# L1's context keys made before L0's expert tiles, and fewer buffers in L1's self-attention

## The chip, the cores and the metric
The kernel runs on one core of a Trainium2 chip. Its metric is device time in microseconds of one execution. Five engines work side by side: PE multiplies matrices into PSUM (its weight loads are shown as PEld), DVE and ACT work on vectors and empty PSUM, POOL does vector work and issues indirect (gathering and scattering) DMAs, and SP issues the plain DMAs. Each engine takes its instructions strictly in the order of its own queue, and waits for the others by semaphores.

## The reference
A decoder of four layers, L0 to L3, is applied to x (8 sequences of 256 tokens, width 256, f32) with a context of 8 x 77 tokens of width 256. Each layer is self-attention, cross-attention and a feed-forward part, each added to x and followed by a layer norm:

```
x = _layernorm(x + _L0_xattn_ref(x, ctx_1024, ...), axis=-1)   # 16 heads of 64
x = _layernorm(x + _L0_ffn_ref(x, ...), axis=-1)               # 8 experts, top 2
x = _layernorm(x + _L1_attn_ref(x, ...), axis=-1)              # 16 heads of 16, causal
x = _layernorm(x + _L1_xattn_ref(x, ctx_1024, ctx_1024, mask_BxSxS2_bk1, ...), axis=-1)  # 16 heads of 64
```

What matters here: the keys of L1's cross-attention are `ctx @ Wk + bk`, 1024 features for 616 context tokens. They depend on inputs alone and not on x, so they can be made at any time. The other stages (L1_ffn, L2, L3) are not touched.

## The kernel before, in words
All activations stay in on-chip memory: x as 16 tiles of 128 tokens (`X`), its transpose as 4 blocks of 512 tokens (`XT`), the transposed context as `cT` (128 x 2 x 616). The stages run one after the other in program order, each opening its own memory pools and closing them at its end, so a later stage's tiles lie on memory of an earlier one. A framework tracks the tiles, adds the semaphore waits, and settles the order of instructions within each engine's queue; a planned program has one fixed order per engine. Results of a batch that need not be finished at once are put on a list (`later`) and advanced by `tick` while the next batch is worked on; `settle` finishes them.

Weights go through one ring of five buffers (`load_w`, tag "w", L172): a load waits until the buffer five loads earlier is no longer read. The plain loads are issued on SP's queue. PSUM is a ring of eight banks (`ps`).

The stages around the change are these.

*L0's cross-attention* (`cross64`, L827) loads Wk, Wq, Wv and Wo, makes the keys `kT` (L839 to L850: sixteen groups of two products `ps<-cT,w` 128x308, each emptied by DVE or ACT in turn), then takes the eight batches: queries (8 groups of 128x256), scores (L894), softmax, weighing, output product, layer norm, and for each batch the routing to experts.

*L0's expert stage* (`l0_ffn`, L1133) settles the last batch's routing, then `route.tables` (L2577) counts tokens per expert with a product on PE (`rbefore,onesb`) and works the tables out on DVE. With these POOL fetches, by indirect DMA, each tile's weights (`W1`, `W2`, in the ring of five) and its 256 token rows (`gx`); PE transposes the rows (L1073), DVE copies them to `gT`, and PE does the two expert products, with the gelu on ACT between them (L1115, after a table load).

*L1's self-attention* (`l1_attn`, L1210) first clears padded tiles by POOL (L1225 to L1228): four `mxp` tiles (two per parity of the batch) and two `vp` tiles. Meanwhile expert results are gathered (`gy`, L1055), added to x (L2680) and normalised (L182 and L183 on POOL, L255 on DVE). For each batch it makes queries, keys and values, the maxima by query (L1285, into `mxp`), transposes them (L1292) and adds them to the queries (`q2`, L1294), makes the scores by key (L1304, L1307), the exponentials `e` (L1312), and weighs the values with them (L1326) into `oT`, which is emptied by L141 or L143 and taken on by `heads_out` (L1354 onwards). The maxima of the next batch are made before the weighing of this one.

*L1's cross-attention* is `cross64` again, with a bias and a mask: Wk, Wq, Wv and Wo are loaded, the keys are made with their bias (L848: `copy_bias`, DVE L148 and ACT L150 in turn), then the batches follow, with the mask (`mk`, loaded by SP, L887) applied to the scores by L908.

Of the kernel before, what the change touches and what calls it, by code (L numbers as in the profile page):

```python
# [14 lines left out]
AF = mybir.ActivationFunctionType  # L15
# [5 lines left out]
P = 128  # L21
NB = 8
S = 256
# [5 lines left out]
NC = NB * SC  # L29
# [32 lines left out]
class Build:  # L62
    def __init__(self, tc, a, ctx):
        self.tc, self.nc, self.a = tc, tc.nc, a
        self.n = 0
        self.flip = 0
        pool = lambda name, bufs=1, **kw: ctx.enter_context(tc.tile_pool(name=name, bufs=bufs, **kw))
        self.const = pool("const")
        self.xp = pool("xp", 2)
        self.wp = pool("wp", 5)  # L70
        self.sm = pool("sm", 4)
        self.tmp = pool("tmp", 3)
        self.psp = pool("ps", 8, space=PSUM)
        self.dr = pool("dr", 1, space=DRAM)
        self.open_keep = lambda: pool("keep")
        self.keep = None
        self.X = [None] * NT
        self.XT = [None] * NBLK
        self.late = lambda: pool("late")
        self.l3w = None  # L80
        self.n_slot_sets = 0
        self.todo = []
        self.results = None
        self.routed = None
        self.slots = {}
        self.ms = {}
# [737 lines left out]
            self.settle()  # L824


    def cross64(self, pre, bias, mask, row, route):  # L827
        nc, a = self.nc, self.a
        with ExitStack() as ctx:
            w1 = ctx.enter_context(self.tc.tile_pool(name=pre + "1", bufs=1))  # L830
            w2 = ctx.enter_context(self.tc.tile_pool(name=pre + "2", bufs=2))
            w3 = ctx.enter_context(self.tc.tile_pool(name=pre + "3", bufs=3))
            Wk = self.load_w(a[pre + "_Wk"], 2, 1024)
            Wq = self.load_w(a[pre + "_Wq"], 2, 1024)
            Wv = self.load_w(a[pre + "_Wv"], 2, 1024)
            Wo = self.load_w(a[pre + "_Wo"], 8, 256)
            kT = self.t(w1, [P, 8, NC], "kT")
            hc = NC // 2
            for n in range(8):  # L839
                for hf in range(2):  # L840
                    ps = self.ps()
                    self.mm(
                        ps[:, :hc],
                        [(Wk[:, k, n * P : (n + 1) * P], self.cT[:, k, hf * hc : (hf + 1) * hc]) for k in range(2)],
                    )
                    o = kT[:, n, hf * hc : (hf + 1) * hc]
                    if bias:
                        self.copy_bias(o, ps[:, :hc], self.fm("l1x_bk")[:, n : n + 1])  # L848
                    else:
                        self.copy(o, ps[:, :hc])  # L850
            if mask is not None:
                big = self.t(w1, [P, 1], "big")
                nc.vector.memset(big, -8.0e9)
# [279 lines left out]
    def l0_ffn(self, route):  # L1133
        nc, a = self.nc, self.a
        with ExitStack() as ctx:
            w1 = ctx.enter_context(self.tc.tile_pool(name="l0f1", bufs=1))
            w2 = ctx.enter_context(self.tc.tile_pool(name="l0f2", bufs=2))
            b2 = self.t(w1, [8, D], "b2")
            nc.sync.dma_start(b2, a["L0_ffn_b2"])
            self.settle()  # L1140
            route.tables(N0)

            cT = self.t(w1, [8, NT, P], "combT")

            def biased(i):
                po = self.ps()
                for k in range(2):
                    nc.tensor.matmul(po[:, k * D : (k + 1) * D], cT[:, i + k, :], b2, start=True, stop=True)
                for k in range(2):
                    nc.vector.tensor_tensor(self.X[i + k], po[:, k * D : (k + 1) * D], self.X[i + k], ALU.add)  # L1150

            def each(j):
                if j == 1:
                    route.places()
                if j == 3:
                    comb = route.combined(w1)
                    for i in range(0, NT, 4):
                        ps = self.ps()
                        for k in range(4):
                            nc.tensor.transpose(ps[:8, k * P : (k + 1) * P], comb[:, i + k, :], self.ident)  # L1160
                        nc.vector.tensor_copy(cT[:, i : i + 4, :], ps[:8].rearrange("p (k n) -> p k n", k=4))
                if j in (4, 5):
                    biased(2 * (j - 4))

            self.routed_tiles(w2, lambda: w2, U0, N0, route, "L0_ffn", 8, 8, AF.Gelu_apprx_tanh, False, True, each)
            self.collect(route)
            for i in range(4, NT, 2):
                biased(i)
# [41 lines left out]
    def l1_attn(self):  # L1210
        nc, a = self.nc, self.a
        with ExitStack() as ctx:
# [5 lines left out]
            self.slot_rows(2)  # L1218
            bk, bq = self.fm("l1_bk"), self.fm("l1_bq")

            mxps, vps = [], []
            for n in range(2):
                mxps.append([self.t(w1, [P, 4, 4, 32], f"mxp{n}{t}") for t in range(2)])
                for m in mxps[n]:
                    nc.gpsimd.memset(m, 0.0)  # L1225
                v = self.t(w1, [P, 2, H, 32], f"vp{n}")
                nc.gpsimd.memset(v, 0.0)
                nc.gpsimd.memset(v[:, :, :, 16:17], 1.0)  # L1228
                vps.append(v)
# [38 lines left out]

            def shift(b, q, k):

                q2 = self.t(w2, [P, 4, S], "q2")
                for t in range(2):
                    n = P * (t + 1)
                    mxp = mxps[b % 2][t]
                    for gs in ((0, 1, 2, 3),) if t == 0 else ((0, 1), (2, 3)):
                        ps = mats(gs, n)
                        for j in range(4):
                            nc.tensor.matmul(ps[j], self.identb, many(later[:, 2 * P - n :], len(gs)), start=True, stop=False)
                        for i, g in enumerate(gs):
                            for j, r in enumerate(rows):  # L1280
                                nc.tensor.matmul(
                                    ps[j][:, i, :], q[r, g, t * P : (t + 1) * P], k[r, g, :n], start=False, stop=(g == gs[-1])
                                )
                        for j in range(4):
                            self.mark = nc.vector.tensor_reduce(  # L1285
                                mxp[:, gs[0] : gs[-1] + 1, j, 16], ps[j], AX.X, ALU.max, negate=True
                            )
                        self.tick()
                for t in range(2):
                    pt = self.ps().rearrange("p (g s) -> p g s", g=4)  # L1290
                    for g in range(4):
                        nc.tensor.transpose(pt[:, g, :], mxps[b % 2][t][:, g].rearrange("p j d -> p (j d)"), self.ident)  # L1292
                    c = slice(t * P, (t + 1) * P)
                    nc.vector.tensor_tensor(q2[:, :, c], pt, q[:, :, c], ALU.add)  # L1294
                return q2

            def weights(q2, k):

                e = {}
                for c, gs in ((0, (0, 1)), (0, (2, 3)), (1, (0, 1, 2, 3))):  # L1300
                    n = S - c * P
                    ps = mats(gs, n)
                    for j in range(4):
                        nc.tensor.matmul(ps[j], self.causb, many(unit[:, :n], len(gs)), start=True, stop=False)  # L1304
                    for i, g in enumerate(gs):
                        for j, r in enumerate(rows):
                            nc.tensor.matmul(  # L1307
                                ps[j][:, i, :], k[r, g, c * P : (c + 1) * P], q2[r, g, c * P :], start=False, stop=(g == gs[-1])
                            )
                    o = self.t(w2, [P, 4, len(gs), n], "e", bufs=4)  # L1310
                    for j in range(4):
                        nc.scalar.activation(o[:, j], ps[j], AF.Exp, scale=0.25)  # L1312
                    for i, g in enumerate(gs):
                        e[c, g] = o[:, :, i, :]
                    self.tick()
                return e

            def weigh(b, e, v):
                o = self.t(w2, [P, 4, S], "oT")
                for gp in range(2):  # L1320
                    ps = self.ps().rearrange("p (g s) -> p g s", g=2)
                    for i in range(2):
# [1379 lines left out]
def build(tc, a, out, layers=LAYERS):  # L2702
    with ExitStack() as ctx:
# [4 lines left out]
        for l in layers:  # L2708
            if l in ("l0_xattn", "l1_xattn", "l2_xattn"):
                route = Routing(g, int(l[1]))  # L2710
            if l == "l1_ffn":
                l2k = ctx.enter_context(ExitStack())
                g.l2k_pool = l2k.enter_context(tc.tile_pool(name="l2k", bufs=1))
# [8 lines left out]
            elif l in ("l2_xattn", "l0_ffn", "l1_ffn", "l2_ffn"):  # L2722
                getattr(g, l)(route)
            else:
                getattr(g, l)()
            if l == "l2_xattn":
                l2k.close()
            if l == "l3_attn":
# [162 lines left out]
```

## Time and profile before
| | us |
|---|---|
| median of 3 runs | 3623.32 (3618.66 to 3629.59) |
| the profiled execution's own time | 3594.94 |
| its span, first to last instruction | 3593.2 |
| PE busy | 3102.3 (86%) |
| DVE busy | 1834.9 (51%) |
| ACT busy | 1043.6 (29%) |
| POOL busy | 928.1 (26%) |

The mean granted clock of PE over the span is 0.896. In the profile a group or instruction has its engine, its source line, the tiles it writes and reads (`out<-in`), partitions by elements, and the idle time before it with what ended that wait. An f32 product shows as several instructions. In the span, L0's cross-attention begins at 456 us, L0's expert tiles at 786, L1's self-attention at 1087 and L1's cross-attention at 1361. The granted clock (PEclk) is the share of full speed that PE was given in a stretch.

### The profile page before, as it was taken

To read this page: it belongs to the slowest core of one execution; us is meant where nothing else is said; L and a number is where in the kernel's file an instruction comes from. 1 tells how busy PE (TensorE), PEld (TensorE's weight loads), DVE (VectorE), ACT (ScalarE), POOL (GpSimd) and SP (SyncE) were. 2 spreads that over 40 slices of the span, in tenths; PEclk is the share of its full clock that TensorE was granted. 3 is DMA by queue.
4 is the path that set the end of the run, shared out by engine and by line. 5 is a ranking of instruction groups with operands and counts; after the bars stand their busy time and mean duration, and the time that the engine had idled before them with its cause. 6 is when DMAs were issued, how large, how long until landed. Compare 5 with 4: busy or idle time off the path is not lost. (4 is left out here: it accounts for less than half of the span.)

```text
span 3593.2 us, 49384 instructions
## 1 busy us (share of the span) xinstructions
PE 3102.3 (86%) x19146; PEld 2184.7 (61%) x19146; DVE 1834.9 (51%) x4823; ACT 1043.6 (29%) x2343; POOL 928.1 (26%) x1398
## 2 busy tenths in 40 slices
PE   4777589979997998998999999898787997778789
PEld 3444257658875665666555777565555785566556
DVE  7888546631116555776211221566675344677652
ACT  4666322212222332332111111344222111343311
POOL 2222513243314101222000000411343444312351
PEclk6777689979998999988999999999777998888889
DMA  9900100035541000001010333200002552000000
GB/s 338 305 2 1 48 7 19 19 108 181 179 144 47 1 25 25 13 14 60 15 36 0 119 124 119 62 1 8 7 19 83 198 196 77 22 1 7 12 5 19
DMA packets 132127, 239.47 MB, mean 67 GB/s; under 512 B 14568, under 2 KB 103920, under 8 KB 124208
## 3 DMA queue, kind: packets, MB, share of 16 engines
q1 hardware_dynamic: 107632, 136.25, 11.3%
q0 software_dynamic: 23104, 98.95, 7.9%
q8 instruction: 154, 2.52, 0.3%
q10 hardware_dynamic: 1152, 1.05, 0.1%
q14 instruction: 85, 0.70, 0.1%
HBM read 156.52 MB, written 79.69 MB: 66 GB/s over the span
## 5 line engine op out<-in xcount | busy, mean ns | idle before, releaser
L155 PE MATMUL ps<-xt,w 128*128 128x256 f32 (+1 forms) x1408 | 452.9, 472 | 3.3 <-issue 2.9
L155 PE MATMUL ps<-w,hT 128*128 128x256 f32 (+1 forms) x1792 | 397.4, 379 | 0.0
L155 PEld LDWEIGHTS ps<-w,hT 128*128 128x128 f32 (+1 forms) x1792 | 329.9, 186 | 56.5 <-issue 6.0
L155 PE MATMUL ps<-gT,w 128*128 128x256 f32 (+1 forms) x1472 | 357.4, 401 | 5.7 <-ACT gT L143 3.0
L155 PEld LDWEIGHTS ps<-xt,w 128*128 128x128 f32 x1408 | 268.7, 198 | 149.4 <-issue 125.0
L155 PEld LDWEIGHTS ps<-gT,w 128*128 128x128 f32 x1472 | 276.5, 191 | 76.8 <-ACT gT L143 3.9
L155 PE MATMUL ps<-w,oT 128*128 128x256 f32 x768 | 181.9, 390 | 3.3 <-DVE mv L251 1.8
L267 POOL TENSOR_TENSOR xb<-x,rows 128x256 f32<-128x256 f32 x96 | 71.6, 752 | 401.7 <-DVE res L272 393.7
L155 PEld LDWEIGHTS ps<-w,oT 128*128 128x128 f32 x768 | 146.4, 194 | 38.5 <-issue 14.1
L235 PE MATMUL ps<-ident,x 128*128 128x128 f32 x320 | 62.0, 307 | 79.5 <-DVE x L255 59.4
L1115 ACT ACTIVATE hT<-ps,more 128x256 f32<-128x256 f32 x152 | 71.9, 474 | 196.1 <-PE ps L155 196.1
L255 DVE TENSOR_SCALAR x<-res,mv,rs 128x256 f32<-128x256 f32 x128 | 57.4, 449 | 126.9 <-POOL rs L183 126.9
L1126 DVE COPY y<-ps 128x512 f32<-128x512 f32 x41 | 28.3, 690 | 174.7 <-PE ps L155 174.7
L1184 DVE TENSOR_TENSOR hT<-hT,ps 128x512 f32<-128x512 f32 x56 | 38.5, 688 | 154.2 <-PE ps L155 152.7
L677 ACT ACTIVATE e<-ps,nm 128x128 bf16<-128x128 f32 (+1 forms) x256 | 103.9, 458 | 40.1 <-DVE nm L672 24.1
L932 PE MATMUL ps<-ident,P 128*77 128x128 f32 x512 | 90.0, 303 | 25.5 <-POOL P L923 15.7
L1666 POOL TENSOR_TENSOR kpad<-kpad,rows 128x256 f32<-128x256 f32 (+1 forms) x10 | 7.3, 729 | 404.2 <-DVE hu L1615 316.9
L923 POOL TENSOR_TENSOR P<-P,z 128x1232 f32<-128x1232 f32 x24 | 54.1, 2252 | 219.6 <-DVE z L921 214.3
L183 POOL TENSOR_TENSOR rs<-rs,mhalf 128x1 f32<-128x1 f32 x192 | 106.1, 554 | 14.2
L932 PEld LDWEIGHTS ps<-ident,P 128*77 128x77 f32 x512 | 60.7, 157 | 73.4 <-issue 25.5
L947 PE MATMUL ps<-PT,V 77*64 77x256 f32 x512 | 98.5, 446 | 7.5 <-DVE PT L141 4.9
L1180 ACT ACTIVATE hT<-ps 128x512 f32<-128x512 f32 x56 | 33.4, 597 | 237.5 <-PE ps L155 237.5
(655 smaller groups left out, 6319.2 us busy)
## 6 DMA issues: line engine op xcount, KB each, us to landing
l2x<-zero SPq DMA_DIRECT2D x28, 1024.0 KB, 11.3
l0x<-zero SPq DMA_DIRECT2D x16, 1024.0 KB, 11.3
w<-in_L_ffn_rg SPq DMA_DIRECT2D x8, 1024.0 KB, 7.0
w<-in_L_ffn_ru SPq DMA_DIRECT2D x8, 1024.0 KB, 5.0
w<-in_L_ffn_rd SPq DMA_DIRECT2D x8, 1024.0 KB, 5.7
l2e<-y SPq DMA_DIRECT2D x22, 256.0 KB, 2.3
rows<-in_rows SPq DMA_DIRECT2D x9, 544.0 KB, 3.7
l0e<-y SPq DMA_DIRECT2D x19, 256.0 KB, 2.9
```

The lines of the kernel that those rows point to most:

```text
L155: self.nc.tensor.matmul(out, lhsT, rhs, start=(i == 0), stop=(i == last))
L183: self.nc.gpsimd.tensor_tensor(out, out, self.mhalf[: in_.shape[0], :w], ALU.pow)
L235: self.nc.tensor.transpose(ps[:, k * P : (k + 1) * P], x[:, k * P : (k + 1) * P], self.ident)
L255: nc.vector.tensor_scalar(t, r, mv[:, 0:1], rs, ALU.subtract, ALU.mult)
L267: self.nc.gpsimd.tensor_tensor(t, self.X[i], row, ALU.add)
L677: nc.scalar.activation(e[:, : (t + 1) * P], ps[j][:, i, :], AF.Exp, bias=nm[:, t, h : h + 1], accum_out=z[:, t, h : h + 1],)
L923: eng.tensor_tensor(pr, pr, z.unsqueeze(2).to_broadcast([P, H, SC]), ALU.mult)
L932: nc.tensor.transpose(psv[:, m, t * P : (t + 1) * P], Pt[t][:, 2 * n + m, :], self.ident)
L947: nc.tensor.matmul(po[64 * m : 64 * m + 64, :S], V[:, h * 64 : (h + 1) * 64], ahead[n % 2][:, m, :], start=True, stop=True,)
L1115: nc.scalar.activation(hT[:, f + m, :], ps[:, m * 256 : (m + 1) * 256], func, bias=more[:, f + m : f + m + 1])
L1180: nc.scalar.activation(hT[:, f, :], ps, func, **({"bias": bias(f)} if bias else {}))
L1184: nc.vector.tensor_tensor(hT[:, f, :], hT[:, f, :], ps, ALU.mult)
```

## The change
The keys of L1's cross-attention are made at the start of L0's expert stage, after the routing tables' instructions in program order, into a tile `l1kT` (128 x 8 x 616 f32, 19.7 KB a partition). It has a pool of its own, open from before L0's expert stage until the end of L1's cross-attention. All sixteen groups are emptied by ACT, with the bias; DVE takes no part. L1's Wk is loaded right after L0's four cross-attention weights, as a fifth load in the ring. L1's cross-attention neither loads Wk nor makes keys.

To make room, L1's self-attention has fewer buffers: one pair of `mxp` tiles instead of two pairs, one `q2` instead of two, three `e` instead of four, one `oT` instead of two.

```diff
+    def context_keys(self, kT, Wk, copy):
+        hc = NC // 2
+        for n in range(8):
+            for hf in range(2):
+                c = slice(hf * hc, (hf + 1) * hc)
+                ps = self.ps()
+                self.mm(ps[:, :hc], [(Wk[:, k, n * P : (n + 1) * P], self.cT[:, k, c]) for k in range(2)])
+                copy(kT[:, n, c], ps[:, :hc], *([self.fm("l1x_bk")[:, n : n + 1]] if kT is self.l1kT else []))
...
     def cross64(self, pre, bias, mask, row, route):
-            Wk = self.load_w(a[pre + "_Wk"], 2, 1024)
+            Wk = self.load_w(a[pre + "_Wk"], 2, 1024) if not bias else None
...
+            if bias:
+                kT = self.l1kT
+            else:
+                kT = self.t(w1, [P, 8, NC], "kT")
+                self.context_keys(kT, Wk, self.copy)
+                self.l1wk = self.load_w(a["L1_xattn_Wk"], 2, 1024)
...
     def l0_ffn(self, route):
             route.tables(N0)
+            self.l1kT = self.t(self.l1k_pool, [P, 8, NC], "l1kT")
+            self.context_keys(
+                self.l1kT, self.l1wk, lambda o, ps, bias: nc.scalar.activation(o, ps, AF.Identity, bias=bias)
+            )
...
     def l1_attn(self):
-            mxps, vps = [], []
+            mxps, vps = [self.t(w1, [P, 4, 4, 32], f"mxp{t}") for t in range(2)], []
+            for m in mxps:
+                nc.gpsimd.memset(m, 0.0)
             for n in range(2):
-                mxps.append([self.t(w1, [P, 4, 4, 32], f"mxp{n}{t}") for t in range(2)])
-                for m in mxps[n]:
-                    nc.gpsimd.memset(m, 0.0)
...
-                q2 = self.t(w2, [P, 4, S], "q2")
+                q2 = self.t(w2, [P, 4, S], "q2", bufs=1)
-                    mxp = mxps[b % 2][t]
+                    mxp = mxps[t]
...
-                    o = self.t(w2, [P, 4, len(gs), n], "e", bufs=4)
+                    o = self.t(w2, [P, 4, len(gs), n], "e", bufs=3)
...
-                o = self.t(w2, [P, 4, S], "oT")
+                o = self.t(w2, [P, 4, S], "oT", bufs=1)
...
     def build(tc, a, out, layers=LAYERS):
+            if l == "l0_ffn":
+                l1k = ctx.enter_context(ExitStack())
+                g.l1k_pool = l1k.enter_context(tc.tile_pool(name="l1k", bufs=1))
...
+            if l == "l1_xattn":
+                l1k.close()
```

In the planned order of the changed kernel the 32 key products stand on PE behind the count product of the tables and ahead of the first expert tile's transposes; on ACT the 16 evictions stand behind the last routing exponential and ahead of the table load for gelu. On SP, L1's Wk follows L0's Wo, and in L1's cross-attention the first load of L1_ffn (sg) moves ahead of the first two masks. On POOL, tile 2's second weight fetch moves behind tile 4's row gathers, and at the start of L1's self-attention the order of memsets, powers (L183) and gathers is a little different. Apart from these, and from the places of a few small DVE instructions, each engine's order is the same.

More of the change, by code (lines that the diff above doesn't have):

```diff
@@ L82, in __init__ @@
         self.todo = []
+        self.l1kT = None
         self.results = None
@@ L836, in cross64 @@
             Wo = self.load_w(a[pre + "_Wo"], 8, 256)
[L837 to L850, printed above, removed]
+            if bias:
[4 more added lines that the diff above has]
+                self.l1wk = self.load_w(a["L1_xattn_Wk"], 2, 1024)
             if mask is not None:
@@ L1291, in shift @@
                     for g in range(4):
-                        nc.tensor.transpose(pt[:, g, :], mxps[b % 2][t][:, g].rearrange("p j d -> p (j d)"), self.ident)
+                        nc.tensor.transpose(pt[:, g, :], mxps[t][:, g].rearrange("p j d -> p (j d)"), self.ident)
                     c = slice(t * P, (t + 1) * P)
```

## The prediction
> **What bounds the kernel now.** I read the page's head first (span 3593.2 us, PE busy 86%). The chain that ended last gives PE only 8% and does not reach back to the stages changed here, so I went by stretches: the timeline around the start of L1's cross-attention, where the keys are made now, then around the start of L0's expert tiles, where they go, then L1's self-attention between them.
>
> Timeline, start of L1's cross-attention (start, duration, engine, line, operation, idle before it):
> ```profile
> 1361.05 0.20 PEld L235 LDWEIGHTS ps<-ident,x 128*128 128x128 f32 x2 [1.25 <-PE ps L235]
> 1361.33 18.44 PE L155 MATMUL ps<-cT,w 128*128 128x308 f32 x64
> ...
> 1376.70 0.54 DVE L148 TENSOR_SCALAR kT<-ps,fmt 128x308 f32<-128x308 f32 x1 [1.54 <-PE ps L155]
> 1377.74 0.52 ACT L150 ACTIVATE kT<-ps,fmt 128x308 f32<-128x308 f32 x1 [1.55 <-PE ps L155]
> ...
> 1379.61 7.07 PE L155 MATMUL ps<-xt,w 128*128 128x256 f32 x32
> ...
> 1386.61 3.65 PEld L894 LDWEIGHTS ps<-kT,qT 64*128 64x128 f32 x64 [0.33 <-DVE qT L148]
> ```
> PE works through the keys without a break; DVE and ACT wait for it. The queries of batch 0 (x32) follow at once and the scores behind them: here PE alone sets the time.
>
> Timeline, start of L0's expert tiles:
> ```profile
> 767.28 0.19 PE L155 MATMUL ps<-rbefore,onesb 128*128 128x8 bf16 x1 [0.16 <-DVE rbefore L2538]
> ...
> 783.48 0.45 PE L1073 MATMUL ps<-ident,gx 128*128 128x128 f32 x1 [16.01 <-DMA gx<-l0x,trows]
> ...
> 785.34 0.69 DVE L1080 COPY gT<-ps 128x512 f32<-128x512 f32 x1 [11.35 <-PE ps L1073]
> ...
> 786.09 9.06 PE L155 MATMUL ps<-gT,w 128*128 128x256 f32 x28 [0.79 <-DVE gT L1080]
> ...
> 788.32 1.28 ACT L1115 ACT_TABLE_LOAD   x1 [23.59 <-PE ps L155]
> ```
> PE stands still for 16.0 us between the counts of the routing tables and the first gathered rows; ACT has nothing for 23.6 us.
>
> Busy time by stretch, the key block of L0's cross-attention (459-463) and that of L1's (1362-1368) among them (PE, PEld, DVE, ACT, POOL, then PEclk, DMA share, GB/s):
> ```profile
> 459.00:461.00 2.00, 2.00 (x6) 1.37 (x5) 0.48 (x1) 0.03 (x1) 0.00 (x0) 0.60 0.00 0
> 461.00:463.00 2.00, 2.00 (x9) 1.48 (x8) 0.48 (x1) 0.39 (x1) 0.00 (x0) 1.00 0.00 0
> ...
> 735.00:740.00 5.00, 5.00 (x24) 3.89 (x24) 1.54 (x3) 0.74 (x2) 0.00 (x0) 0.50 0.00 0
> ...
> 1362.00:1365.00 3.00, 3.00 (x7) 1.98 (x6) 0.54 (x1) 0.00 (x0) 0.00 (x0) 0.50 0.15 60
> 1365.00:1368.00 3.00, 3.00 (x13) 2.17 (x12) 0.54 (x1) 1.03 (x2) 0.00 (x0) 0.98 0.00 0
> ...
> 786.10:803.20 17.10, 17.10 (x69) 14.57 (x70) 0.69 (x1) 4.92 (x9) 10.37 (x11) 0.84 0.78 282
> 803.20:817.40 14.20, 14.20 (x69) 12.32 (x68) 1.38 (x2) 3.80 (x8) 6.80 (x8) 1.00 0.60 205
> ```
> After a pause the granted clock is 0.50 and comes back to 1.00 after about 4 us of dense work; expert tile 0 takes 17.1 us, tile 1 14.2 us.
>
> Timeline, start of L1's self-attention:
> ```profile
> 1080.94 0.51 POOL L1225 MEMSET mxp<- 128x512 f32 x1
> 1081.01 1.95 DVE L255 TENSOR_SCALAR x<-x,mv,rs 128x256 f32<-128x256 f32 x1 [1.53 <-POOL rs L183]
> 1081.40 0.94 POOL L1227 MEMSET vp<- 128x1024 f32 x1
> 1082.30 0.51 POOL L1225 MEMSET mxp<- 128x512 f32 x1
> ```
> The normalisation that PE waits for takes 1.95 us here instead of 0.41, until POOL's memsets pause.
>
> **Part 1, the keys leave L1's cross-attention.** Sixteen groups of two f32 products (x64 with their passes) go. At full clock a group takes 1.036 us (evictions at 1376.70 and 1377.74), 16 x 1.036 = 16.6; the block takes 18.3 because it began at clock 0.50 (18.3 - 16.6 = 1.7 lost, the price of 3.4 us at half clock). That slow start is inherited by the queries, so I take **-16.6**. Ends: -18.3 if the queries start at full clock; -15.5 if they stay slow for 5.6 us, as expert tile 0 did (786.1 to 791.7), losing 2.8 instead of 1.7. What could be late next: Wq landed long before (issued 1068.71); the mask is issued at 1356.93 and lands in 1.7 us, and its reader moves from 1388.2 to about 1371.6. In SP's queue L1_ffn's first load (sg) now goes ahead of the masks, but it waits for the self-attention's Wv buffer, free at 1324-1326 when the cross-attention's own loads go out: 30 us before the mask. The 16 evictions (8 x 0.538 on DVE, 8 x 0.518 on ACT) were covered by PE and bring nothing by themselves.
>
> **Part 2, they come before L0's expert tiles.** In PE's order they stand behind the count product (767.5) and ahead of tile 0's transposes. From a cold start they end at 767.5 + 16.6 + (1.7 to 2.8) = 785.8 to 786.9, later than the rows arrive (783.5). Four transposes (0.60 at full clock) and the copy to gT (0.69, 0.1 of latency) put tile 0 at 787.2 to 788.3, 1.1 to 2.2 after 786.09. But PE then comes warm: tile 0 at tile 1's 14.25 instead of 17.1 ends at 801.5 to 802.6 against 803.2. I take **-1.0**, ends -1.7 and, if the clock falls back before tile 0, +2.2. ACT's 16 evictions (0.518 each, one per 1.036) end some 0.5 us behind PE, ahead of the table load, which waits for tile 0's first product anyway. The tables are DVE work and untouched. POOL's first sixteen fetches keep their order; W1 of tile 2 now also waits for the keys (free at 787, issued at 792.32 before), and W2 of tile 2 goes behind tile 4's row gathers, issued at 797.16 either way because it waits for tile 0. Nothing.
>
> [...]
>
> **Part 3, the extra load.** L1's Wk (1 MB) follows Wo in SP's queue and waits for ACT's last read (L406) of the fourth block at 430.7; the next load behind it, the rows, was issued at 448.45 for a reason of its own (POOL L267). Wk lands in 4.9 us: **0**, both ends 0. With it all five weight buffers are taken; the first expert's fetches take Wk's and Wq's buffers, read last before 760, and go out from 774.78.
>
> **Part 4, fewer buffers in L1's self-attention.** Every reader of a reused buffer stands earlier in PE's queue than the products that feed its next writer. The nearest: the last weighing product (L1326) of batch 6 ends at 1338.4, the first exponential of batch 7 writes at 1340.50, 2.1 us later. ACT gets about two more waits a batch on work of its own long done; a semaphore step is 0.05 us in the trace: 16 x 0.05 = 0.8 at most. I take **0**, ends 0 and +0.8.
>
> **Part 5, memsets at its start.** Two of the four mxp memsets (0.52) go, but the order becomes mxp, vp, vp, and a gather (0.95 + 0.30 to the next) slips ahead of the second power (L183). The memsets now run unbroken to 1083.2 instead of 1082.8, so the first normalisation ends 0.4 later; the second power starts about 1.3 later, but its scaling is no longer held up 0.6: **+0.7**, ends -1.0 (the memset time saved) and +1.3. PE waits for both (1083.01, 1086.24), and the later gathers, which start after batch 0's maxima (1110.06), move along.
>
> [...]
>
> **Sum:** -16.6 - 1.0 + 0 + 0 + 0.7 = **-16.9 us**. The profiled execution took 3594.94 us (span 3593.2 plus 1.7), 0.8% below the median of the runs, 3623.32; I take the same microseconds off the median: **3606.4**. The ends of the terms add up to -21.0 and -11.2: 3602 to 3612.
>
> **Rivals.** (a) *The keys don't get the full clock in their new place.* For it: 735-740, PE busy all the time at 0.50, and so until 751. Against: both key blocks in the trace reached 1.00 after 4 us, as dense there as here. At 0.50 throughout they take 33.1 and end at 800.6; tile 0 would start at 802.0 and end at 816.3, 13.1 late: -16.6 + 13.1 + 0.7 = -2.8, 3620.5, no change. Chance 0.13.
> (b) *Self-attention is serialised by its single buffers* (slower). Place: the hand-over between batches, if the weighing of a batch fell behind the next scores. Price: 64 weighing products 2.81, the copy to oT 0.69, its eight transposes 1.09: 4.6 x 7 = 32; 32 - 16.9 = +15, 3638.6. It costs more than the keys bring from 2.4 us a hand-over, and is slower by 0.3% from 4.0. For it: four buffers are cut at once. Against: PE's order does not change and 2.1 us are spare. Chance 0.08.
> (c) *Part of the gain is given back in small clock losses*: each pause after which PE restarts at 0.50 costs 1.7 to 2.8, and shifted stages meet the clock at other moments. Four such losses (9) leave -8, 3615, no change. Chance 0.09.
>
> **How the numbers follow.** The forecast has 0.70. About 0.3% (10.9 us) is what a measurement of this kernel can tell from no change. Faster: the forecast and a little of (c), 0.73; same: (a), the rest of (c), 0.18; slower: (b) and what I do not see, 0.09. The range takes the terms' ends, 3602 to 3612, widened by the scatter of the runs shown (3618.66 to 3629.59, 5 either way) and half of (c): 3598 to 3617.
>
> **What would show it.** Right: score products of L1's cross-attention some 16.6 us nearer to the end of the self-attention, no 128x308 products there; the 16 us wait before the first expert transposes gone and tile 0 at clock 1.00; stretches of the self-attention of equal length. Wrong: the key block longer than 20 us at 0.50; tile 1 starting after 805; ACT's exponentials waiting for L1326; a wait for the mask or Wq before the first scores.

## The result and the profile after

The changed kernel took 3614.66 us (median of 18 runs, 3611.25 to 3619.58) against 3624.51 for the kernel before on the same chip (18 runs, 3618.04 to 3629.59): ratio 0.9976, 95% interval 0.9970 to 0.9983. That is 9.9 us faster, inside the 0.3% called no change, where 16.9 were forecast.

The same two kernels were later run in six more sessions, each on one chip, and the sessions fall into two kinds: in the first kind before takes about 3596 us, in the second 3616 to 3625. The profile on record for before (3594.94) is of the first kind, the profiled run of after (3617.24, span 3615.5) of the second. The two are therefore compared by stretches here.

Timeline of after, PE only, at the start of L0's expert tiles (start, duration, engine, line, operation, idle before it):
```profile
775.52 0.19 PE L156 MATMUL ps<-rbefore,onesb 128*128 128x8 bf16 x1 [0.17 <-DVE rbefore L2544]
775.62 18.94 PE L156 MATMUL ps<-cT,w 128*128 128x308 f32 x64
794.39 0.60 PE L1075 MATMUL ps<-ident,gx 128*128 128x128 f32 x4
804.60 9.25 PE L156 MATMUL ps<-gT,w 128*128 128x256 f32 x28 [9.60 <-ACT l1kT L1147]
...
821.89 7.07 PE L156 MATMUL ps<-gT,w 128*128 128x256 f32 x32
```
The keys run from the count product on without a break, as forecast, and the four transposes follow at once: the rows are there. Then PE stands still for 9.60 us. From the count product to tile 1 it is 46.37 us (821.89 - 775.52); in the profile of before it was 35.92 (803.20 - 767.28).

The same stretch on ACT, then on DVE and POOL:
```profile
783.19 0.52 ACT L1147 ACTIVATE l1kT<-ps,fmt 128x308 f32<-128x308 f32 x1 [0.52 <-PE ps L156]
...
786.56 0.52 ACT L1147 ACTIVATE l1kT<-ps,fmt 128x308 f32<-128x308 f32 x1 [1.63 <-PE ps L156]
...
792.25 0.52 ACT L1147 ACTIVATE l1kT<-ps,fmt 128x308 f32<-128x308 f32 x1 [1.62 <-PE ps L156]
797.18 0.52 ACT L1147 ACTIVATE l1kT<-ps,fmt 128x308 f32<-128x308 f32 x1 [4.41 <-remote]
802.80 0.52 ACT L1147 ACTIVATE l1kT<-ps,fmt 128x308 f32<-128x308 f32 x1 [5.11 <-remote]
803.54 1.74 ACT L1147 ACTIVATE l1kT<-ps,fmt 128x308 f32<-128x308 f32 x4 [0.22 <-remote]
```
```profile
803.80 0.69 DVE L1082 COPY gT<-ps 128x512 f32<-128x512 f32 x1 [21.56 <-remote]
```
```profile
783.03 0.96 POOL L1039 DMA_INDIRECT w<-in_L_ffn_W1t,twrow  x1 [0.30 <-DMA l0x<-x,rto]
...
803.95 0.94 POOL L1039 DMA_INDIRECT w<-in_L_ffn_W1t,twrow  x1 [3.70 <-remote]
```
The keys' products ended at 794.6, but ACT empties the last six groups between 797 and 805. DVE copies `gT` 8.8 us after its transposes (794.39 + 0.60). Three engines, each waiting for PE, are let go within half a microsecond, at 803.5 to 803.95. "remote" means that the signal they waited for came at a moment when no instruction in the trace ended: PE's work was done (it had gone on to the next products), its completion signals were late. How late shows group by group: the block of keys ends at 794.56, and at full clock a group takes 1.036 us. ACT starts the first five evictions 0.04 us after their group's products end. The fetch of tile 0's first weights is issued at 783.03, and from the next group on the delay grows: 0.2, 1.3, 1.7, 2.8, 3.9, 7.8 and, for the twelfth group, 12.4 us (790.41 to 802.80).

Busy time of after in this stretch (PE, PEld, DVE, ACT, POOL, then PEclk, DMA share, GB/s):
```profile
787.00:789.00 2.00, 2.00 (x10) 1.45 (x9) 0.00 (x0) 0.59 (x2) 1.69 (x2) 1.00 0.86 315
...
795.00:797.00 2.00, 0.00 (x0) 0.00 (x0) 0.00 (x0) 0.00 (x0) 1.39 (x3) 1.00 0.99 406
797.00:799.00 2.00, 0.00 (x0) 0.00 (x0) 0.00 (x0) 0.52 (x1) 1.70 (x2) 1.00 0.93 360
...
803.00:805.00 2.00, 0.40 (x1) 0.43 (x2) 0.69 (x1) 1.78 (x5) 0.94 (x1) 0.50 0.00 0
```
While the signals are late, the weights and rows of tiles 0 and 1 arrive at 207 to 406 GB/s (stretches of 2 us from 787 to 801). The signals are through again when that traffic ends (DMA share 0.13 from 801 to 803). By then the clock is back at 0.50, so tile 0 is cold once more (821.89 - 804.60 = 17.3 us).

Timeline of after, PE only, at the start of L1's cross-attention:
```profile
1374.49 1.99 PE L156 MATMUL ps<-w,oT 128*128 128x256 f32 x8
...
1381.17 8.50 PE L156 MATMUL ps<-xt,w 128*128 128x256 f32 x32
1389.60 2.57 PE L896 MATMUL ps<-l1kT,qT 64*128 64x77 f32 x42
```
The block of 128x308 products is gone. The queries inherit its cold start (8.50 us instead of 7.07, granted clock 0.62 until 1385 and 1.00 from there), and the scores follow.

Timeline of after, start of L1's self-attention:
```profile
1099.61 2.38 DVE L256 TENSOR_SCALAR x<-x,mv,rs 128x256 f32<-128x256 f32 x1 [0.98 <-POOL rs L184]
1099.99 1.83 POOL L1233 MEMSET vp<- 128x1024 f32 x2
```
The first normalisation takes 2.38 us instead of 1.95: the 0.4 of the prediction.

### The profile page after: what moved, and what is told of

Its sections match the earlier page's. It is cut to its first block, busy times and chain, and to the rows that moved or that the text cites. A ratio compares the mean times of both kernels' runs of the same rounds, so it can differ in the third digit from the quotient of the medians.

```text
span 3615.5 us, 49376 instructions
## 1 busy us (share of the span) xinstructions
PE 3125.2 (86%) x19135; PEld 2200.5 (61%) x19146; DVE 1825.0 (50%) x4815; ACT 1048.6 (29%) x2351; POOL 926.7 (26%) x1396
```

## The experiments

**What are the parts worth?** Two theories: A, Part 2 is right and the gain was lost elsewhere (in self-attention, or Part 1 is worth less); B, the gain is lost beside the gathers. One kernel makes the keys in both places, another has the fewer buffers alone; the two original kernels run beside them.

Keys made twice (L1's Wk is loaded again as well):
```diff
-            Wk = self.load_w(a[pre + "_Wk"], 2, 1024) if not bias else None
+            Wk = self.load_w(a[pre + "_Wk"], 2, 1024)
...
                 kT = self.l1kT
+                self.context_keys(kT, Wk, self.copy_bias)
```
Fewer buffers alone (L1's Wk is loaded in its old place):
```diff
...
-                kT = self.l1kT
+                kT = self.l1kT = self.t(w1, [P, 8, NC], "kT")
+                self.context_keys(kT, Wk, self.copy_bias)
...
-                self.l1wk = self.load_w(a["L1_xattn_Wk"], 2, 1024)
...
-            self.context_keys(
-                self.l1kT, self.l1wk, lambda o, ps, bias: nc.scalar.activation(o, ps, AF.Identity, bias=bias)
-            )
```
Before, unchanged: 

> The kernel before, unchanged, for a second trace, because the profiled execution of before (3594.94 us) lies 29.6 under the median of its runs (3624.5) and the stages that the change does not touch stand 8.2 us (L0's cross-attention), 3 to 5 us (L2's routing) and 11 us (L2's experts) later in the trace of after. If those differences are the granted clock of one execution, this trace is longer than 3593 and its L0 cross-attention takes about as long as in after (first query product to count product 299.2, not 292.0); the key block of L1 takes 18 to 19 again and PE again waits about 16 us before tile 0. If they belong to the change, this trace repeats 3593 +- 5 and 292.0.

After, unchanged: 

> The changed kernel, unchanged, on the same chip as the next two. If PE's wait of 9.6 us between tile 0's transposes and its first product (ACT's last key evictions, DVE's copy of gT and POOL's fetch all held until 803.5) belongs to the keys standing beside the gathers, it is there again, 5 to 12 us long; if it was an accident of one execution, tile 0 starts within 2 us of its transposes and count product to tile 1 takes 34 to 36 us. Time against before: -10 either way.

Keys twice: 

> L1's keys are made in both places (the later ones overwrite the earlier with the same values). Against after it prices Part 1, against the next kernel Parts 2 and 3. Theory A (my sum, Part 2 right, the gain was lost elsewhere): 15.5 to 18.3 slower than after if Part 1 is right and about 8 if Part 1 is where the gain was lost. Theory B (the gain is lost beside the gathers, Part 1 right): 15.5 to 18.3 slower than after, so 5 to 8 slower than before.

Fewer buffers: 

> Only the fewer buffers of L1's self-attention: the keys stay where they were in before, no early block, no extra load. My sum for Parts 4 and 5: +0.7 (ends -1.0 and +2.1) against before. Theory A (loss in self-attention): +7. Theory B (loss beside the gathers): +0.7 here, and keys_twice minus this +7 to +10; by my sum keys_twice minus this would be -1.0.

| kernel | median us | ratio to before (3596.03), 95% |
|---|---|---|
| before | 3597.80 | 1.0005 (0.9996 to 1.0014) |
| after | 3580.26 | 0.9958 (0.9944 to 0.9971) |
| keys twice | 3598.18 | 1.0004 (0.9995 to 1.0013) |
| fewer buffers | 3599.14 | 1.0003 (0.9994 to 1.0012) |

Here the change brought 15.8 us, where -10 had been expected, and neither theory's loss is there. In the trace of after every eviction of the keys starts 0.04 us after its products. Keys twice less after is 17.9 (Part 1, forecast 15.5 to 18.3); keys twice less fewer buffers is -1.0 (Parts 2 and 3, forecast -1.0), less than the 3 us either way of each median's interval. PE in the trace of after:
```profile
767.46 0.19 PE L156 MATMUL ps<-rbefore,onesb 128*128 128x8 bf16 x1 [0.16 <-DVE rbefore L2544]
767.56 18.65 PE L156 MATMUL ps<-cT,w 128*128 128x308 f32 x64
786.04 0.60 PE L1075 MATMUL ps<-ident,gx 128*128 128x128 f32 x4
787.47 6.37 PE L156 MATMUL ps<-gT,w 128*128 128x256 f32 x28 [0.83 <-ACT l1kT L1147]
...
801.89 4.48 PE L156 MATMUL ps<-gT,w 128*128 128x256 f32 x20
```
The key block is as long as in the first trace of after (18.65 and 18.94), but tile 0 starts at 787.47, warm (granted clock 1.00 from 786 to 792, in the trace of before beside it 0.50), and tile 1 at 801.89: the prediction's 787.2 to 788.3 and 801.5 to 802.6. The 9.6 us wait is a matter of the session, not of the kernel's order alone. The trace of before repeats the one on record (span 3595.5).

What else differs between the two kinds is seen in a view of DMA issues, of the first trace of after and of this one (count, then median us from issue to landing):
```profile
gx<-l0x,trows POOLq DMA_INDIRECT x38
```
```profile
gx<-l0x,trows POOLq DMA_INDIRECT x38, 4.6
```
The first has no landing time, because some landing signals are missing from that trace. The same holds for PE's signals: in the trace of the result's session 3393 updates of PE's semaphore are recorded for 3442 signalling products, in this one 3446 (a few come from elsewhere). Of DMA landings the one trace has 7649 records, the other 10325.

**In a session of the other kind.** Before took 3616.30 here. Theory B now reads: in some sessions the signals of PE's products come late while the first gathers of an expert stage run, and the change puts the keys beside them. Theory C: the ratios are scatter, with no tie to the wait. Two kernels test it: half of the keys early and half in their old place (L1's Wk is loaded again for them); and all keys early, but tile 1's weights and tile 2's rows fetched only once tile 0's rows are in `gT`.
```diff
-                self.l1kT, self.l1wk, lambda o, ps, bias: nc.scalar.activation(o, ps, AF.Identity, bias=bias)
+                self.l1kT, self.l1wk, lambda o, ps, bias: nc.scalar.activation(o, ps, AF.Identity, bias=bias), range(4)
...
                 kT = self.l1kT
+                self.context_keys(kT, Wk, self.copy_bias, range(4, 8))
```
```diff
-        experts[start + 1] = fetch(start + 1)
-        xs[start + 2] = fetch_x(start + 2)
         each(-1)
         pool = pool()
         gT = self.turned(px, xs[start], experts[start][2], scale)
+        self.held = self.gT_made if table == "L0_ffn" and start == 0 else None
+        experts[start + 1] = fetch(start + 1)
+        xs[start + 2] = fetch_x(start + 2)
+        self.held = None
```
(`held` is an instruction that the fetches are made to depend on.)

Before, for a trace (one run, 3620.40 us): 

> The kernel before once more, for a trace on the chip of this batch. The two chips so far differ: 3624.5 for before on the first, 3596.0 on the second. If this is a chip like the first, the trace shows whether before too has PE's signals late in the first burst of gathers of an expert stage (L2's experts at least, as in the trace of after there: 9.6 us), and whether tile 0's transposes of L0 are followed by gT within 1 us. If it is like the second, it repeats 3593 to 3599 with no such wait.

After: 

> The changed kernel on the chip of this batch. Theory B (on some chips the signals of PE's products come late while the gathers run, and the keys stand beside them): on a chip where before takes about 3624, -8 to -11 against before and again 5 to 10 us of waiting between tile 0's transposes and first product; on one where before takes about 3596, -15 to -17 and a wait under 1 us. Theory C (the two ratios so far are the scatter of single sessions): anything between, with no tie to the wait.

Half of the keys: 

> Half of the keys (8 groups) early, the other half at the start of L1's cross-attention. The early half ends at 777.5 to 778.6, before the weight gathers' traffic is at its height, and PE then waits cold for the rows. By my sum: -8.3 (half of Part 1) + 0 (tile 0 starts as in before) + 0.7 = -7.6 against before, on any chip. Theory B: the same, with no late signal at tile 0, so on a chip like the first about as good as the whole change (-8 to -11), on one like the second 8 slower than it.

Tile 1's fetches held: 

> The changed kernel with tile 1's weights and tile 2's rows fetched only after tile 0's rows are copied to gT: 2.6 MB less traffic beside the keys, all keys still there. Theory B: on a chip like the first the wait at tile 0 shrinks from 9.6 to under 5 and the time falls by as much against after; on one like the second it is the same as after within 2 us, for tile 1's weights (issued at about 790, 6 us to landing) are still there before 801.7. If they come late, tile 1 waits for W1 and it is slower.

| kernel | median us | ratio to before (3616.30), 95% |
|---|---|---|
| after | 3610.43 | 0.9989 (0.9979 to 0.9999) |
| half of the keys | 3616.99 | 1.0000 (0.9990 to 1.0011) |
| tile 1's fetches held | 3604.25 | 0.9970 (0.9958 to 0.9982) |

PE in the traces of before, of after, and with tile 1's fetches held:
```profile
772.27 0.19 PE L155 MATMUL ps<-rbefore,onesb 128*128 128x8 bf16 x1 [0.16 <-DVE rbefore L2538]
788.45 1.18 PE L1073 MATMUL ps<-ident,gx 128*128 128x128 f32 x4 [15.99 <-DMA gx<-l0x,trows]
790.42 7.71 PE L155 MATMUL ps<-gT,w 128*128 128x256 f32 x28 [0.78 <-DVE gT L1080]
...
801.02 1.13 PE L155 MATMUL ps<-gT,w 128*128 128x256 f32 x4 [2.02 <-ACT hT L1115]
...
808.46 2.75 PE L155 MATMUL ps<-gT,w 128*128 128x256 f32 x12
```
```profile
768.94 0.19 PE L156 MATMUL ps<-rbefore,onesb 128*128 128x8 bf16 x1 [0.16 <-DVE rbefore L2544]
769.04 18.98 PE L156 MATMUL ps<-cT,w 128*128 128x308 f32 x64
787.86 0.60 PE L1075 MATMUL ps<-ident,gx 128*128 128x128 f32 x4
797.90 7.66 PE L156 MATMUL ps<-gT,w 128*128 128x256 f32 x28 [9.45 <-ACT l1kT L1147]
...
813.61 3.62 PE L156 MATMUL ps<-gT,w 128*128 128x256 f32 x16
```
```profile
772.09 0.19 PE L157 MATMUL ps<-rbefore,onesb 128*128 128x8 bf16 x1 [0.16 <-DVE rbefore L2552]
772.18 18.97 PE L157 MATMUL ps<-cT,w 128*128 128x308 f32 x64
790.99 0.60 PE L1081 MATMUL ps<-ident,gx 128*128 128x128 f32 x4
792.42 6.37 PE L157 MATMUL ps<-gT,w 128*128 128x256 f32 x28 [0.83 <-ACT l1kT L1155]
...
806.84 1.89 PE L157 MATMUL ps<-gT,w 128*128 128x256 f32 x8
811.64 5.45 PE L157 MATMUL ps<-gT,w 128*128 128x256 f32 x24 [2.91 <-ACT hT L1125]
```
The wait is back in after (9.45), and before does not have it: PE is idle while the first of the fetches run, and `gT` follows its transposes as usual; its longest wait within tile 0 is 2.02 us. From the count product to tile 1 it is 36.19 in before, 44.67 in after (+8.5) and 34.75 with tile 1's fetches held (-1.4). Up to there the last differs from after only in the traffic beside the keys, and it gains 6.2 us by the medians (the two intervals overlap by little). That speaks for B and against C. ACT's evictions with tile 1's fetches held say more:
```profile
788.70 3.01 ACT L1155 ACTIVATE l1kT<-ps,fmt 128x308 f32<-128x308 f32 x7 [2.31 <-PE ps L157]
```
With tile 0's weights and the rows of tiles 0 and 1 alone beside the keys the signals are late too, by up to 3.8 us at the tenth group (products done at 784.93). Then the fetches end (DMA share 0.95 from 785 to 787, 0 from 789), ACT catches up, and the last eviction is 0.04 us behind again. But with POOL issuing the fetches of tiles 1 and 2 without a pause from 792.6 to 808.6, a wait of 2.91 appears in tile 1.

Half of the keys missed: -7.6 expected, nothing measured. Its trace falls short in two places. Tile 1 starts 38.31 us after the count product, 36.19 in before; it was to start as in before. L1's first queries stand at 1377.67 against 1384.82, but 2.4 of these 7.2 us were there already at the count product (769.84 against 772.27), so 4.7 are gained up to here. Then that gain melts while the order of work stays the same: in 1450 to 1500 us the granted clock is 0.86, in before 1.00, and by 1670 (the Wo product at 1669.81 against 1672.88) 0.6 of it is left. Clock of half of the keys, then of before, in these 50 us:
```profile
1450.00:1500.00 50.00, 47.32 (x298) 34.02 (x294) 34.43 (x118) 16.62 (x38) 11.85 (x15) 0.86 0.04 12
```
```profile
1450.00:1500.00 50.00, 44.62 (x292) 31.25 (x292) 35.92 (x117) 18.20 (x42) 12.62 (x18) 1.00 0.04 12
```
The second of these is rival (c), clock losses that give a gain back, met in another kernel than the one it was written for. One trace shows it; that it sets the median is not shown.

**Is it traffic of two tiles at once?** The next kernel also holds tile 2's weights and tile 3's rows, until tile 0's result is copied out:
```diff
+            self.held = self.tile_end.ins if table == "L0_ffn" and start == 0 and j == 0 else None
             xs[j + 3] = fetch_x(j + 3)
             experts[j + 2] = fetch(j + 2)
+            self.held = None
             each(j)
```


> The changed kernel on the chip of this batch, beside the next. Theory B: with before near 3596, -15 to -17 and less than 1 us of waiting at tile 0; with before at 3616 or more, -5 to -11 and 9 to 10 us of waiting there. A chip in between tells whether the wait comes and goes or grows.

> The changed kernel with tile 1's weights held until tile 0's rows are in gT (as in the run before), and tile 2's weights and tile 3's rows until tile 0's result is copied out, so that no two tiles' weights travel at once while PE works. Theory B: on a chip with late signals the 2.9 us wait that the later burst put into tile 1 (POOL had issued W1 and W2 of tile 1 and of tile 2 within 12 us) goes too, and the time is 8 to 11 below the changed kernel, 15 to 17 below before; on a chip without late signals the same as the changed kernel within 2. If tile 2's weights (issued at about 803, 6 us to landing, needed at about 816) are late, it is slower than the run with tile 1 alone held back.

The same kernels in three further sessions:

> The changed kernel on the chip of this batch. As before under theory B: with before at 3616 or more, -5 to -11 and 9 to 10 us of waiting at tile 0; with before near 3596, -15 to -17 and under 1 us.

> The same kernel with the fetches spread (the last one of the run before, unchanged), wanted on a chip with late signals. Theory B: there 8 to 11 below the changed kernel; no wait over 1 us between tile 0's transposes and its products, and none over 1 us in tile 1. If the late signals come from PE's own dense work and not from the fetches beside it, spreading them changes nothing and it is within 2 of the changed kernel. On a chip without late signals it is the same as the changed kernel within 2 either way.

> The changed kernel on the chip of this batch. Theory B: with before at 3616 or more, -5 to -11 and 9 to 10 us of waiting at tile 0; with before near 3596, -15 to -17 and under 1 us.

> Tile 1's weights and tile 2's rows held until tile 0's rows are in gT, unchanged from the run before. Theory B: on a chip with late signals about 6 below the changed kernel, with the wait at tile 0 under 1 us and one of some 3 us in tile 1; on another chip the same as the changed kernel within 2.

> Tile 2's weights held back as well. Theory B: on a chip with late signals 8 to 11 below the changed kernel, and no wait over 1 us in tiles 0 and 1. If the late signals follow PE's dense work wherever the first fetches fall, the wait only moves to tile 2 and this is no better than holding tile 1 alone. On another chip the same as the changed kernel within 2.

> The changed kernel on the chip of this batch. Theory B: with before at 3616 or more, -5 to -11 and 9 to 10 us of waiting at tile 0; with before near 3596, -14 to -17 and under 1 us.

> The fetches of tiles 1 and 2 held back, unchanged. Theory B: on a chip with late signals 8 to 11 below the changed kernel and no wait over 1 us in tiles 0 and 1; on another chip the same within 2.

| before, median us | after | tile 1 held | tiles 1 and 2 held |
|---|---|---|---|
| 3596.01 | 3580.97, 0.9953 (0.9939 to 0.9967) | | 3581.31, 0.9950 (0.9936 to 0.9964) |
| 3596.70 | 3582.79, 0.9960 (0.9946 to 0.9973) | | 3581.68, 0.9958 (0.9944 to 0.9972) |
| 3596.72 | 3582.35, 0.9962 (0.9948 to 0.9975) | 3582.22, 0.9961 (0.9948 to 0.9975) | 3579.67, 0.9954 (0.9941 to 0.9968) |
| 3622.84 | 3615.12, 0.9976 (0.9966 to 0.9985) | | 3612.44, 0.9973 (0.9962 to 0.9985) |

In the three sessions of the first kind all versions are alike, as every theory said, and the gain is 13.9 to 15.0, at the low end of what was expected. In the fourth after gains 7.7 and has the wait again (9.58 us). With both tiles held the 8 to 11 hoped for are not there: 2.7, and the intervals lie over each other. PE and DVE in its trace:
```profile
793.76 6.37 PE L157 MATMUL ps<-gT,w 128*128 128x256 f32 x28 [0.83 <-ACT l1kT L1157]
...
808.18 7.07 PE L157 MATMUL ps<-gT,w 128*128 128x256 f32 x32
...
822.43 1.89 PE L157 MATMUL ps<-gT,w 128*128 128x256 f32 x8
828.60 7.13 PE L157 MATMUL ps<-gT,w 128*128 128x256 f32 x24 [4.28 <-issue]
```
```profile
827.96 0.69 DVE L1136 COPY y<-ps 128x512 f32<-128x512 f32 x1 [10.78 <-remote]
```
Tiles 0 and 1 run without a wait; the wait, 4.28 us, now stands in tile 2. Holding tile 2's fetches made tile 3's follow them without a pause: POOL issued both from 809.3 to 825.3, then again waited for a late signal. So in these traces of after and of the held fetches the wait stands where two tiles' fetches run together beside PE's products (9.45 and 9.58 us at tile 0, 2.91 in tile 1, 4.28 in tile 2), and holding back the first moved it. In tiles 0 and 1 of this trace one tile's fetches at a time led to no wait, though beside the keys tile 0's alone made signals up to 4.1 us late.

No version beat the changed kernel in both kinds of session beyond the intervals; holding tile 1 alone was ahead of it in the one session with late signals where it ran, and level in the other. The wait at the keys is thus tied to the fetches beside them; what would take it away without moving it was not found.

## Why the prediction was wrong

- **Part 2, "I take -1.0, ends -1.7 and, if the clock falls back before tile 0, +2.2"**, is the step that failed. In the session of the first kind that has traces of both, count product to tile 1 went from 36.00 (before) to 34.43, so -1.6: start, warm tile and end came as worked out. In the result's session the term was far off: +10.4 against the profile on record; within one session with late signals it was +8.5 at tile 1 and +7.4 at tile 3's transposes (65.85 against 58.46 us after the count product), since before loses 1.1 of its own between the two. The keys were not too slow (18.94) and the rows not late. The sum put the hand-over at next to nothing: "ACT's 16 evictions ... end some 0.5 us behind PE" and the copy to `gT` with "0.1 of latency". In the result's session the last eviction started 10.2 us behind its products, the copy 8.8, and the prediction's own sign, a late tile 1, came (821.89, where 805 was the limit), with a key block under 20 us. The trace that I had could not show it: PE was idle during the first of those fetches, and in sessions of its kind the signals come at once even beside them (ACT within 0.04 us of each group).
- **"I take the same microseconds off the median"**: the gap of 3594.94 to 3623.32 was noted and then passed over. It was the sign that the profile and the runs were of two kinds of session, in one of which signals are late.
- **Part 1, -16.6**: right. From the last Wo product of self-attention to the first scores: 31.73 in before (1357.39 to 1389.12) and 15.14 in after (1355.37 to 1370.51) in the session of the keys made twice, so -16.6; 15.11 in the result's session (1374.49 to 1389.60). The queries inherit the cold start: 8.69 and 8.50 us in these two traces of after, 7.07 in before.
- **Part 3, 0**: nothing in the traces waits for the load; keys twice less fewer buffers, -1.0, holds it together with Part 2, but is too small to be told from 0.
- **Part 4, 0**: right for the buffers. In the trace of fewer buffers the self-attention, first products to L1's keys, takes 273.67 us, in two of before 273.94 and 273.57. With the keys moved it is 274.7 to 275.1 (to L1's queries), in the same kind of session: in batch 1 PE waits 2.0 to 2.3 instead of 0.9 to 1.1 us for DVE's `vp`. None of the buffers taken away is involved there; why that wait grows stays open.
- **Part 5, +0.7**: right in size. From tile 3's transposes to the first products 263.0 and 263.4 in before, 263.7 with fewer buffers, 263.7 to 264.3 in after.
- **Rivals.** (a): no, in the result's session the clock is 0.50 until 779, 0.78 to 781 and 1.00 from then to the end of the keys. (b): no, as under Part 4. (c) is the nearest in size (3615 forecast, 3614.66 measured), but the loss came from elsewhere: one wait of 9.6 us and tile 0's cold start after it (clock 0.50 at its beginning, 17.3 us for the tile). That wait was no rival of mine. That 3614.66 still lies in the range of 3598 to 3617 is luck: the range was widened for (c) and for scatter, not for this.

With Part 2 at +7.4, Part 1 at -16.6 and Parts 4 and 5 at the +1.9 of the traces, the sum is -7.3; the three sessions with late signals gave -9.9, -5.9 and -7.7. With -1.6 it is -16.3; the four others gave -15.8, -15.0, -13.9 and -14.4. The rest, up to 2.6 us either way, was not traced to a place.

## What to carry to other kernels

Before an engine's gap is filled, ask what else moves in that gap, above all gathers: the hand-over of the new work to the other engines is part of its cost (here a wait of 9.60 us in the result's session, 0.83 in the next). If the profiled execution lies well away from the median of the runs (here 3594.94 against 3623.32), it may be of another kind of session; compare a second trace before taking its microseconds off the median. What a change gains in one stage is to be looked for at the end of the later ones too: in the one trace of half of the keys 4.7 us were gained at L1's first queries and 0.6 of it was left by 1670, with the clock at 0.86 in 1450 to 1500 us where before had 1.00.

## What the runs showed of the hardware

In three of seven sessions the completion signals of PE came late while an expert stage's weights were fetched beside dense f32 products: by up to 12.4, 12.3 and 13.1 us in the block of keys in the three traces of after, by up to 3.8 and 4.1 where tile 1's weights were held. In all five of these traces ACT takes up the first five groups within 0.04 us, and the sixth, the first late one, ends 1.2 to 1.3 us after the issue of tile 0's first weights. In the nine traces of the other four sessions that make all the keys there, each of the sixteen groups is taken up within 0.04 us, beside fetches of the same size. It is not bound to the change: in the trace of before with late signals the start of L2's expert tiles has the same, 8.69 us, where the other kind waits 1.31. Before with late signals, then before without:
```profile
2808.78 6.70 PE L155 MATMUL ps<-xrs,l2s 128*128 128x512 f32 x9 [8.69 <-issue]
```
```profile
2791.85 7.13 PE L155 MATMUL ps<-xrs,l2s 128*128 128x512 f32 x16 [1.31 <-DVE xrs L1846]
```
Why some sessions have it stays open. The record gives the same chip number, 2, for the third session of the first kind in the last table and, some five minutes later, for the one of the second kind, so a chip of that number is not of one kind for good. All seven traces with late signals lack many signal records: 3390 to 3406 of PE's for 3440 to 3442 products, and 7649 to 7888 DMA landings. The other twelve lack at most one of PE's and have 10316 to 10341 landings. Each timed execution comes with a span and a granted clock, so each seems to have been recorded, and whether the wait exists without recording was not tried: how much of the 9.6 us a kernel that nobody records would lose is not known.
